# A two-layer graph network on one core: layer 2's partial sums kept in DRAM between the layers, in place of a second projection in layer 1

## The chip, the cores and the metric

The kernel runs on one core of one Trainium2 chip. The core has a matrix engine (TensorE; PE in the profile, with PEld for its weight loads), a vector engine (VectorE, DVE), a scalar engine (ScalarE, ACT), GpSimd (POOL), and SyncE (SP), which issues DMAs; 16 DMA engines move the data. Each engine works through its own instructions in program order and waits on semaphores. The metric is the time of one execution in microseconds (us), the median of several runs.

## The reference

There are N = 12500 nodes with 128 features and E = 200000 edges sorted by their target `dst`. Each edge has one of ten relations, the place of the largest of ten attributes. Both layers have the same form:

```python
def _rgcn_layer(x, src, dst, edge_type, w_rel, root, bias):
    N = x.shape[0]
    seg = dst * NUM_REL + edge_type
    xs = x[src]
    sums = jax.ops.segment_sum(xs, seg, num_segments=N * NUM_REL)
    cnt = jax.ops.segment_sum(jnp.ones(seg.shape, x.dtype), seg, num_segments=N * NUM_REL)
    mean = (sums / jnp.maximum(cnt, 1.0)[:, None]).reshape(N, NUM_REL, -1)
    return jnp.einsum('nrd,rdo->no', mean, w_rel) + x @ root + bias
...
h = jax.nn.relu(_rgcn_layer(x, src, dst, edge_type, w_rel1, root1, b1))
return _rgcn_layer(h, src, dst, edge_type, w_rel2, root2, b2)
...
x = _layernorm(x + _L0_gnn_ref(...), axis=-1)
```

So for each node and relation the rows of its neighbours are averaged, each average is multiplied by the relation's 128 x 128 matrix, and the ten results are added. Layer 2 does this with h, the rows that layer 1 gives. The sum over a node's edges may be split: the sums of two parts of the edges may be projected one by one, or added first and projected once.

## The kernel before, in words

**Tiles of edges.** The edges are cut into 1563 tiles of 128. For each tile GpSimd issues one indirect DMA (`gathered`, L751) that fetches the 128 source rows. VectorE builds one-hot columns for target and relation (`ones`, L765 for layer 1's edges, L768 for compacted ones), ScalarE weights them with 1 / count (`weighted`, L757), TensorE multiplies rows and one-hots into a PSUM bank `zp` (L978 in layer 1, L1480 in layer 2), and VectorE adds the bank into an accumulator `cc` (`sum_into`, L792) at a column that depends on the tile's first node.

**The accumulator.** `cc` is `[128, 2, 10, 1024 + 120]` floats: two rings, ten relations each, with one column for each of 1024 consecutive nodes (the columns after 1024 catch what runs over the end, and `folded` adds them to the beginning). As the nodes move on, a block of 256 nodes (128 or fewer near the end) that is complete is projected: `projected` multiplies the ten relations' columns by the ten weights (L739; one float product shows as two instructions) and adds one more product (L742). Then `cleared` (ScalarE, L722, two halves of five relations) writes zeros, and the same columns serve the nodes that lie 1024 further on.

**Layer 1 does part of layer 2.** From tile T0 = 166 on, the gather fetches from `XH`, a table that holds x and, for nodes whose h is ready, h next to it (zeros otherwise). So one gather of 1 KB rows feeds two products: x into ring 0 for layer 1, and h into ring 1 for layer 2. An edge whose source had its h in time is called seen. When a block k is complete, `finish` (L839) queues its steps at later positions of the tile loop, in units of four tiles: `rows_out` (bias, ReLU, transposition), `rows_kept` (h to `hD` and to `XH`), `second` (L876: projection of ring 1's sums over seen edges with layer 2's weights, and of h with its root matrix), `second_kept` (L879: bias by ScalarE, L883, and a store to `T2`, L884), the clears of both rings, and the next block's fetch.

**Layer 2** (`layer_2`, L1289) handles what is left: the first 166 tiles, and the unseen edges, which `brought_together` (L1058) sorts into 695 compacted tiles (using ring 0 as scratch, then zeroing it). These tiles form two walks, one from node 0 with ring 1, one from about node 6800 with ring 0, and a planner takes tiles from both in turn (`taken_in_turns`). Wide tiles are done in several passes over columns. `done_at` and `free_until` give the position at which a block is complete and at which its ring columns are needed again. `finish` (L1392) projects the block and adds the row of `T2` through a product with the identity (L742), `turn` transposes, `norm` adds x, normalises and stores `out`; two clears (8 and 12 units after the projection, a unit being 0.7 gathers for a block of 256 nodes) free the columns. `fetched` loads the block's rows of x and of `T2` on SyncE's queue. The block in which the walks meet (`partial`, `final`) goes through `T2` once more.

**Order.** The instructions are issued in the order written (a manual schedule). Waits follow from declared ranges: `offsets` (L773) reads a tile's column into a register and declares the range that it can have. A tile whose possible nodes lie on both sides of a multiple of 1024 is declared as the whole ring:

```python
lims = [limits(t0 + j) for j in range(n)]
lims = [(lo % RN, hi % RN) if lo // RN == hi // RN else (0, RN - 1) for lo, hi in lims]
```

A sum with a declared range waits for every earlier instruction or DMA that touches a column in it. There are 7 gather buffers of 8 rows each (a pair of x and h takes two), 6 for one-hots, and 3 (layer 2) or 5 (layer 1) PSUM banks for `zp`.

## Time and profile before

| | |
|---|---|
| median of 3 runs | 3114.19 us (3112.14 to 3119.51) |
| profiled execution, its own time | 3108.35 us |
| its span, first to last instruction | 3106.5 us |
| mean granted TensorE clock | 0.84 |
| layer 1's gathers | from the start to about 1958 us |
| layer 2's gathers | 1969.45 to about 3052 us |
| moved by DMA | 370.97 MB |

In the rows of groups, a name such as `zp<-oh,g` tells what is written from what; after `x` stands the number of instructions, then their busy time and the mean of one in ns, and behind the second bar the idle time of the engine just before them with what ended it ("issue": nothing that the profile shows). In the rows of windows each engine has its busy time and its number of instructions in brackets, in the order PE, PEld, DVE, ACT, POOL (a window of fewer engines or one line has those alone), then the granted clock, the DMA engines' busy share and GB/s. In a timeline the columns are start, duration, engine, line, operation, and in brackets the idle time before and what ended it. In the rows of waits stand the total, the number and the longest.

### The profile page before, as it was taken

What the parts mean: (1) busy time and instruction counts of PE and PEld (TensorE: products, weight loads), DVE (VectorE), ACT (ScalarE), POOL (GpSimd) and SP (SyncE); (2) the same over time, 40 slices, a digit from 0 to 9 for tenths busy, and PEclk for the clock granted to TensorE, in tenths of its full rate; (3) what the DMA queues carried; (4) which work ended last, traced back from release to release, by engine and by line L of the source; (5) the groups of instructions that cost most, each with busy time, mean ns of one, the idle gap of its engine ahead of it and who ended that gap; (6) DMA issues with size and microseconds to landing.
All of it is one profiled execution on the core that took longest, in us unless ns stands there. A gap on an engine that the chain in (4) does not pass through costs nothing.

```text
span 3106.5 us, 42362 instructions
## 1 busy us (share of the span) xinstructions
PE 2368.2 (76%) x11861; PEld 1949.5 (63%) x11861; DVE 2031.1 (65%) x5465; ACT 1301.6 (42%) x3177; POOL 2295.8 (74%) x2436
## 2 busy tenths in 40 slices
PE   2768787888787878787878788546467777777887
PEld 1556677777776767676767677545445555555665
DVE  6764657665656767655646464597776676777766
ACT  3533443433333434333433333332434455555643
POOL 7777777777777777777777777677777777777772
PEclk8768888888888889888888888767788888998988
DMA  6874444444545454545454444322222222222221
GB/s 191 270 216 143 141 145 141 140 146 122 161 122 162 124 157 129 159 122 160 125 158 127 128 121 118 95 59 62 64 67 68 72 73 74 72 73 73 79 73 43
DMA packets 265199, 370.97 MB, mean 119 GB/s; under 512 B 51232, under 2 KB 197189, under 8 KB 264958
## 3 DMA queue, kind: packets, MB, share of 16 engines
q0 software_dynamic: 99920, 250.57, 29.4%
q1 hardware_dynamic: 111347, 91.97, 9.4%
q10 hardware_dynamic: 53691, 25.62, 2.8%
q8 instruction: 102, 1.67, 0.2%
q14 instruction: 139, 1.14, 0.1%
HBM read 322.86 MB, written 57.89 MB: 123 GB/s over the span
## 4 chain that ended last, share of the span: by engine, by line
PE 30%; POOL 22%; issue 19%; DVE 14%; DMA 10%; ACT 2%; DVEq 1%; ACTq 0%; POOLq 0%; SPq 0%
POOL g L751 22%; PE pf L739 13%; DMA g<-XH,idxE 9%; PE zp L978 8%; PE zp L1480 6%; DVE cc L792 5%; DVE oh L768 2%; PE pf L742 1%; DVE cc L1158 1%; DVEq L777 1%; ACT cc L722 1%; ACT oh L757 1%; DVE oh L765 1%; DVE st L703 1%; DVE go L1146 1%
## 5 line engine op out<-in xcount | busy, mean ns | idle before, releaser
L751 POOL DMA_INDIRECT g<-XH,idxE x1397 | 1321.2, 946 | 425.6 <-issue 384.8
L792 DVE TENSOR_TENSOR cc<-cc,zp 128x240 f32 (+13 forms) x2500 | 959.8, 384 | 777.8 <-PE zp L978 388.2
L978 PE MATMUL zp<-oh,g 128*128 128x120 f32 x5920 | 983.2, 318 | 370.5 <-DMA g<-XH,idxE 206.8
L978 PEld LDWEIGHTS zp<-oh,g 128*128 128x128 f32 x5920 | 866.5, 222 | 487.2 <-issue 184.8
L751 POOL DMA_INDIRECT g<-hD,idxB x695 | 657.3, 946 | 215.9 <-issue 195.3
L739 PE MATMUL pf<-cc,w 128*128 128x256 f32 (+4 forms) x3000 | 732.1, 405 | 18.9 <-DVE cc L792 15.1
L1480 PE MATMUL zp<-oh,g 128*128 128x120 f32 (+23 forms) x1874 | 507.3, 415 | 284.4 <-DVE cc L792 156.4
L739 PEld LDWEIGHTS pf<-cc,w 128*128 128x128 f32 x3000 | 610.4, 215 | 121.1 <-DVE cc L792 22.5
L1480 PEld LDWEIGHTS zp<-oh,g 128*128 128x128 f32 x1874 | 338.9, 227 | 430.9 <-issue 271.0
L757 ACT ACTIVATE oh<-oh,wE 128x120 f32<-128x120 f32 x1729 | 530.9, 383 | 186.0 <-DVE oh L765 139.4
L757 ACT ACTIVATE oh<-oh,wB 128x150 f32<-128x150 f32 (+23 forms) x771 | 339.1, 482 | 296.5 <-DVE oh L768 269.4
L722 ACT ACTIVATE cc<-zero 128x1280 f32<-128x1280 f32 (+3 forms) x274 | 336.6, 1231 | 85.3 <-DVE cc L792 81.5
L768 DVE TENSOR_TENSOR oh<-go,keyB 128x480 f32<-128x480 f32 (+20 forms) x476 | 260.3, 547 | 115.1 <-PE zp L1480 113.6
L672 ACT ACTIVATE a<-pf,b 128x256 f32<-128x256 f32 (+1 forms) x50 | 23.3, 465 | 580.6 <-PE pf L742 578.9
L765 DVE TENSOR_TENSOR oh<-bank,keyE 128x480 f32<-128x480 f32 x391 | 253.0, 647 | 0.0
L751 POOL DMA_INDIRECT g<-hD,idxE x166 | 158.8, 957 | 61.7 <-issue 46.0
L751 POOL DMA_INDIRECT g<-in_x_dram,idxE x166 | 156.9, 945 | 52.2 <-issue 47.9
L883 ACT ACTIVATE v<-pf,b 128x256 f32<-128x256 f32 (+2 forms) x52 | 23.9, 459 | 361.4 <-PE pf L742 333.2
L548 DVE TENSOR_TENSOR eqb<-bank,kh 128x1344 bf16<-128x1344 f32 (+2 forms) x65 | 100.4, 1549 | 2.4 <-PE pf L559 2.0
L557 PE MATMUL pf<-eqb,identb 128*128 128x512 bf16 (+2 forms) x130 | 58.9, 453 | 12.4 <-DVE eqb L548 12.4
L559 PE MATMUL pf<-eqb,identb 128*128 128x512 bf16 (+2 forms) x130 | 58.5, 450 | 0.0
L706 ACT ACTIVATE rstd<-mv,eps 128x2 f32<-128x2 f32 (+5 forms) x54 | 15.9, 295 | 83.8 <-DVE mv L704 83.3
(235 smaller groups left out, 1097.8 us busy)
## 6 DMA issues: line engine op xcount, KB each, us to landing
m<-in_edge_attr_dram SPq DMA_DIRECT2D x48, 672.0 KB
g<-XH,idxE POOLq DMA_INDIRECT x1397
XH<-in_x_dram ACTq DMA_DIRECT2D x24, 512.0 KB
XH<-zero ACTq DMA_DIRECT2D x24, 512.0 KB
XH<-hb SPq DMA_DIRECT2D x87, 128.0 KB
g<-hD,idxB POOLq DMA_INDIRECT x695
xb<-in_x_dram SPq DMA_DIRECT2D x72, 128.0 KB
out_dram<-o SPq DMA_DIRECT2D x47, 128.0 KB
```

Of the source, the lines that this page charges most:

```text
L548: nc.vector.tensor_tensor(eq[:p], kpP[:p, None, :R].to_broadcast([p, DB, R]), fore, op=ALU.is_equal)
L557: nc.tensor.matmul(pc[:p], identb[:p, :p], eq[:p, k:k + 4, L:], start=(d + k == 1), stop=False)
L559: nc.tensor.matmul(pc[:p], identb[:p, :p], back, start=False, stop=(d + k + 3 == L))
L722: nc.scalar.activation(cc[:, l, h * H:(h + 1) * H, o:o + n], zero[:, None, :n].to_broadcast([P, H, n]), AF.Copy)
L739: nc.tensor.matmul(po[:, :n], wsb[l][:, r, :], cc[:, l if ring is None else ring, r, o:o + n], start=(r == 0), stop=False)
L751: nc.gpsimd.indirect_dma_start(out=g[:, j * C:(j + n) * C], out_offset=None, in_=table, in_offset=bass.IndirectOffsetOnAxis(ap=idx, axis=0))
L757: nc.scalar.activation(s, s, AF.Copy, scale=w)
L765: nc.vector.tensor_tensor(o.rearrange("p (t m) -> p t m", m=m), cols[:, None, :m].to_broadcast([P, n, m]), keys[:, :, None].to_broadcast([ ...
L768: nc.vector.tensor_tensor(o.rearrange("p (t r n) -> p t r n", r=NREL, n=w), cols[:, None, :, :w].to_broadcast([P, n, NREL, w]), keys[:, :, ...
L792: nc.vector.tensor_tensor(s, s, z, op=ALU.add)
L978: nc.tensor.matmul(zp[:, a + l * KW:a + (l + 1) * KW], g[:, (slot[j] + l) * C:(slot[j] + l + 1) * C], oh[:, j * KW:(j + 1) * KW], start=Tr ...
L1480: nc.tensor.matmul(zp[:, j * m:(j + 1) * m], gt[:, b * C:(b + 1) * C], oh[:, j * m:(j + 1) * m], start=True, stop=True)
```

## The change

In layer 1 `second` and `second_kept` are gone. In their place `sums_kept`, three parts (12 gathers) after the block's projection, stores h as columns in `hT` and, for blocks that can have seen edges, the block's columns of ring 1 in `S2`, `[128, 10, N]` in DRAM, both on SyncE's queue.

In layer 2 the clears are gone. `sums_back` loads the columns of `S2` for the nodes 1024 further on into the projected block's place, 2 units after the projection. Ring 0 gets its first 852 nodes from `S2` once the sorting has zeroed it. The projection then covers all edges at once: it adds root times h in place of identity times `T2`, `turn` adds the bias, and `final` adds the other walk's part by one more product with the identity. `T2` holds that one part alone. Tiles of the pool `fin` for up to four groups of 128 rows become tiles for three (left out of the diff, as are the lines around).

```diff
--- before.py
+++ after.py
@@ -208,7 +208,8 @@
     hD = dram.tile([N, C], F32, name="hD")
     hT = dram.tile([C, N], F32, name="hT")
     XH = [dram.tile([N, 2 * C], F32, name=f"XH{i}") for i in range(2)]
-    T2 = dram.tile([C, N], F32, name="T2")
+    S2 = dram.tile([C, NREL, N], F32, name="S2")
+    T2 = dram.tile([C, YB], F32, name="T2")
     KD = dram.tile([1, L + NT * P + L], F32, name="KD")
     CN = dram.tile([1, NT * P], F32, name="CN")
     counts = dram.tile([RS, NPAD], F32, name="counts")
...
@@ -729,17 +730,16 @@
         nc.vector.tensor_tensor(s, s, e, op=ALU.add)
         nc.vector.memset(e, 0.0)
 
-    def projected(k, l, last, po=None, more=True, ring=None):
+    def projected(k, l, ring, lasts):
 
         n0, n, _ = block(k)
         o = n0 % RN
-        if po is None:
-            po = ps_f.tile([P, YB], F32, name="pf")
-        for r in range(NREL if more else 0):
-            nc.tensor.matmul(po[:, :n], wsb[l][:, r, :], cc[:, l if ring is None else ring, r, o:o + n],
-                             start=(r == 0), stop=False)
-        w, f = last
-        nc.tensor.matmul(po[:, :n], w, f[:, :n], start=not more, stop=True)
+        po = ps_f.tile([P, YB], F32, name="pf")
+        for r in range(NREL):
+            nc.tensor.matmul(po[:, :n], wsb[l][:, r, :], cc[:, ring, r, o:o + n],
+                             start=(r == 0), stop=(r == NREL - 1 and not lasts))
+        for i, (w, f, a, b) in enumerate(lasts):
+            nc.tensor.matmul(po[:, a:b], w, f[:, :b - a], start=False, stop=(i == len(lasts) - 1))
         return po
 
     def stored(hb, b, k):
@@ -845,16 +845,16 @@
                 fTs[k] = features_in(k, 0, xbs[k])
             u = QB if t < NT else 0
             folded(ALL, k, WN)
-            po = [projected(k, 0, (rsb[0], fTs[k]))]
+            n0, n, subs = block(k)
+            po = [projected(k, 0, 0, [(rsb[0], fTs[k], 0, n)])]
             both = starts[k + 1] > bounds(T0)[0] if k + 1 < NBLK else True
             reused = starts[k] + RN < N
             assert not reused or t + 7 * u <= (starts[k] + RN - OFF - WN) // STEP
 
             def rows_out(_):
-                a = po.pop()
-                a = fin_a.setdefault(k, shifted(a, k, 0))
+                a = shifted(po.pop(), k, 0)
                 pr = ps_f.tile([P, 4, C], F32, name="pf")
-                n0, n, subs = block(k)
+                hs.append(a)
                 for i, h in subs:
                     nc.tensor.transpose(pr[:h, i, :], a[:, i * P:i * P + h], ident)
                 po.append(pr)
@@ -873,29 +873,23 @@
                         when = t + 8 * QB if k < K0 else first_seen[k] + 2 * QB
                         todo_late.append((when, lambda t: stored(hb, 1 - first, k)))
 
-            def second(_):
-                po.append(projected(k, 1, (rsb[1], fin_a.pop(k)), more=both))
-
-            def second_kept(_):
-                n0, n, _ = block(k)
-                p2 = po.pop()
-                t2 = fin.tile([P, YB], F32, name="v")
-                nc.scalar.activation(t2[:, :n], p2[:, :n], AF.Identity, bias=bsb[1])
-                nc.sync.dma_start(T2[:, n0:n0 + n], t2[:, :n])
+            hs = []
+
+            def sums_kept(_):
+                nc.sync.dma_start(hT[:, n0:n0 + n], hs.pop()[:, :n])
+                if both:
+                    o = n0 % RN
+                    nc.sync.dma_start(S2[:, :, n0:n0 + n], cc[:, 1, :, o:o + n])
 
             todo.at(t + u, rows_out)
             todo.at(t + (1 if k == NBLK - 2 else 2) * u, rows_kept)
             if reused:
                 todo.at(t + 2 * u, lambda t: cleared(0, k, 0))
                 todo.at(t + 3 * u, lambda t: cleared(0, k, 1))
-            if k < NBLK - 1:
-                todo.at(t + (9 if k >= NBLK - 3 else 3) * u, second)
-                todo.at(t + (9 if k >= NBLK - 3 else 4) * u, second_kept)
-            else:
+            if k == NBLK - 1:
                 todo.run(t)
                 todo.run(END)
-                todo.at(t, second)
-                todo.at(t, second_kept)
+            todo.at(t + 3 * u, sums_kept)
             if both:
                 w = 10 if k >= NBLK - 3 else 5
                 todo.at(t + w * u, lambda t: cleared(1, k, 0))
@@ -914,14 +908,13 @@
                 def turned_kept(t):
                     n0, n, subs = block(k + 1)
                     pt = po.pop()
-                    fTs[k + 1] = fin.tile([P, 4 * P], F32, name="fT")
+                    fTs[k + 1] = fin.tile([P, 3 * P], F32, name="fT")
                     nc.scalar.activation(fTs[k + 1][:, :n], pt[:, :n], AF.Copy)
                 todo.at(t + u, fetch)
                 w = 2 if k == NBLK - 3 else 4
                 todo.at(t + w * u, turn)
                 todo.at(t + (w + 1) * u, turned_kept)
 
-        fin_a = {}
         todo_late = []
         xbs[0] = rows_in(0)
         fTs[0] = features_in(0, 0, xbs[0])
@@ -1382,12 +1375,26 @@
                 return
             n0, n, subs = block(k)
             tail = "e" if walk_of[k] or k == final else ""
-            if k != partial:
-                assert k != final or partial in ended
-                xbs[k] = (comp if tail else fin).tile([P, 4, C], F32, name="xb" + tail)
+            if k == partial:
+                fTs[k] = None
+                return
+            if k == final:
+                assert partial in ended
+                fTs[NB2] = comp.tile([P, ranges[-1][partial][1]], F32, name="fP")
+                nc.sync.dma_start(fTs[NB2], T2[:, :ranges[-1][partial][1]])
+            if True:
+                xbs[k] = (comp if tail else fin).tile([P, 3, C], F32, name="xb" + tail)
                 rows_dma(xbs[k], x, k, False)
-            fTs[k] = (comp if tail else fin).tile([P, 4 * P], F32, name="fT" + tail)
-            nc.sync.dma_start(fTs[k][:, :n], T2[:, n0:n0 + n])
+            fTs[k] = (comp if tail else fin).tile([P, 3 * P], F32, name="fT" + tail)
+            nc.sync.dma_start(fTs[k][:, :n], hT[:, n0:n0 + n])
+
+        def sums_back(l, a, b):
+
+            ring = 1 - l
+            while a < min(b, (shared[1], N)[l]):
+                e = min(b, (shared[1], N)[l], a // RN * RN + RN)
+                nc.sync.dma_start(cc[:, ring, :, a % RN:a % RN + e - a], S2[:, :, a:e])
+                a = e
 
         def finish(k, i):
 
@@ -1398,7 +1405,10 @@
             u = (1 if n > YB * 5 // 8 else 0.7) if i < NG else 0
             folded(slice(ring, ring + 1), k, max([b[6] for b, (lo, hi) in zip(bunches, reaches)
                                                   if b[0] == walk_of[k] and lo < n0 < hi] + [WN]))
-            po = [projected(k, 1, (ident, fTs[k]), ring=ring)]
+            lasts = [] if k == partial else [(rsb[1], fTs[k], 0, n)]
+            if k == final:
+                lasts.insert(0, (ident, fTs[NB2], n - ranges[-1][partial][1], n))
+            po = [projected(k, 1, ring, lasts)]
             following = turn_of[walk_of[k]]
             if k == partial:
                 following = turn_of[1][1:2]
@@ -1410,12 +1420,13 @@
                 following = []
 
             def turn(_):
-                a = fin.tile([P, YB], F32, name="a")
-                nc.scalar.activation(a[:, :n], po.pop()[:, :n], AF.Copy)
+                a = fin.tile([P, 3 * P], F32, name="a")
                 if k == partial:
-                    nc.sync.dma_start(T2[:, n0:n0 + n], a[:, :n])
+                    nc.scalar.activation(a[:, :n], po.pop()[:, :n], AF.Copy)
+                    nc.sync.dma_start(T2[:, :n], a[:, :n])
                     fetched(following[0])
                     return
+                nc.scalar.activation(a[:, :n], po.pop()[:, :n], AF.Identity, bias=bsb[1])
                 pr = ps_f.tile([P, 4, C], F32, name="pf")
                 for b, h in subs:
                     nc.tensor.transpose(pr[:h, b, :], a[:, b * P:b * P + h], ident)
@@ -1430,8 +1441,7 @@
             assert i < by, (k, i, by)
             todo.at(min(i + 6 * u, by), turn)
             if clear[k]:
-                todo.at(min(i + 8 * u, by), lambda i: cleared(ring, k, 0))
-                todo.at(min(i + 12 * u, by), lambda i: cleared(ring, k, 1))
+                todo.at(min(i + 2 * u, by), lambda i: sums_back(1 - ring, n0 + RN, n0 + n + RN))
             if k != partial:
                 todo.at(i + 10 * u, norm)
 
@@ -1486,10 +1496,13 @@
                 flagged()
                 flag = 0
             jobs.run(i)
+            if "ring" in ready and "sums" not in ready:
+                ready.add("sums")
+                sums_back(1, shared[1], shared[0] + RN)
             q = p - BE
             if q >= 0:
                 l, second, t0, n, w, c, whole = bunches[q]
-                assert not l or "ring" in ready
+                assert not l or "sums" in ready
                 for j in range(n):
                     t = t0 + j
                     if (second, t) not in offs:
```

10 lines of the change are left out of this document (5 added, 5 removed).

## The prediction

> **What bounds the kernel now.** I read the page first (parts 1, 5 and 3), then windows by stage, then the waits of GpSimd and of VectorE, then two timelines.
>
> ```profile
> span 3106.5 us, 42362 instructions
> PE 2368.2 (76%) x11861; PEld 1949.5 (63%) x11861; DVE 2031.1 (65%) x5465; ACT 1301.6 (42%) x3177; POOL 2295.8 (74%) x2436
> L751 POOL DMA_INDIRECT g<-XH,idxE x1397 | 1321.2, 946 | 425.6 <-issue 384.8
> L739 PE MATMUL pf<-cc,w 128*128 128x256 f32 (+4 forms) x3000 | 732.1, 405 | 18.9 <-DVE cc L792 15.1
> ...
> L883 ACT ACTIVATE v<-pf,b 128x256 f32<-128x256 f32 (+2 forms) x52 | 23.9, 459 | 361.4 <-PE pf L742 333.2
> ```
>
> No engine is full by its share of busy time. The gather row says why that misleads: each gather is 946 ns of work and 0.30 us of "issue" (425.6 / 1397), and while it issues nothing else holds GpSimd back. The windows of all engines over layer 1 (250 to 1900) and the steady part of layer 2, and GpSimd's waits over the whole span, say it again:
>
> ```profile
> 250.00:1900.00 1650.00, 1356.55 (x7515) 1175.37 (x7513) 1019.37 (x2728) 641.70 (x1655) 1247.85 (x1321) 0.85 0.48 139
> 2200.00:3051.00 851.00, 643.40 (x2518) 465.65 (x2519) 604.71 (x1724) 432.42 (x901) 640.41 (x678) 0.88 0.28 72
> POOL g L751 <- issue: 674.0, 2212, 0.3
> POOL g L751 <- PE zp L978: 24.7, 81, 0.3
> POOL g L751 <- PE zp L1480: 16.0, 39, 2.3
> POOL g L751 <- PE pf L742: 14.4, 11, 11.4
> ```
>
> 1650 / 1321 is 1.249 us for one gather, which is 0.946 + 0.30: in layer 1 GpSimd never stops. Its longest wait there is 0.3 us. So **layer 1 lasts as long as its gathers**, whatever TensorE does beside them, as long as TensorE keeps up (1356.55 of 1650 busy).
>
> Layer 2 is different. The last gather and the product that uses it:
>
> ```profile
> 3050.91 0.94 POOL L751 DMA_INDIRECT g<-hD,idxB  x1 [0.30 <-issue]
> 3089.70 0.58 PE L1480 MATMUL zp<-oh,g 128*128 128x250 f32 x2
> 1969.45 0.94 POOL L751 DMA_INDIRECT g<-hD,idxE  x1 [11.38 <-PE pf L742]
> 1976.53 1.93 PE L1480 MATMUL zp<-oh,g 128*128 128x120 f32 x10 [2.49 <-ACT oh L757]
> ```
>
> The first layer 2 product runs 7.1 us behind its gather, the last one 38.8 us behind. TensorE and VectorE have fallen behind the gathers, and after 3051 they still work for 55 us. **The end of the kernel is set by the consumers of layer 2**, not by GpSimd: time added to their chain moves the end, and time taken out moves it by up to 38.8 - 7.1 = 31.7 us, when GpSimd becomes the bound.
>
> **Layer 1: what goes and what comes.** The second projection goes: it is 20 of the instructions of L739 for each of the 48 blocks from node 1024 on, 960 of 3000, or 732.1 x 960 / 3000 = 234 us of TensorE, with the 52 `second_kept` of L883 (23.9 us of ScalarE). All of it lies beside the gathers, at 1.249 us each: I cost the removal at **0**. If that cover were not there, the 234 us would be the gain; the 0.3 us waits exclude it.
>
> In its place SyncE stores 128 x 10 x 256 floats for each block (1.31 MB; 11476 nodes x 5120 bytes = 58.8 MB in all), and the same comes back in layer 2.
>
> ```profile
> q1 hardware_dynamic: 111347, 91.97, 9.4%
> 100.00:250.00 150.00, 112.18 (x547) 90.90 (x546) 92.83 (x242) 68.66 (x191) 113.42 (x121) 0.78 0.75 226
> 1500.00:1750.00 250.00, 210.18 (x1130) 180.66 (x1131) 135.75 (x307) 94.11 (x244) 189.07 (x201) 0.83 0.47 135
> ```
>
> SyncE's queue moved 91.97 MB in 9.4% of 3106.5 us, 0.315 MB in a us, so one store takes 1.31 / 0.315 = 4.2 us of all 16 DMA engines and all stores 187 us, a tenth of layer 1: the share goes from 0.47 to about 0.57. At 0.75 the gathers ran at 150 / 121 = 1.24 us, as at 0.47. Behind the store wait `cleared(1, k)` on ScalarE, due 2 parts (8 gathers, 10 us) later, and any sum whose declared range covers the block; both have 4 to 7 us to lose at most, and the gather buffers hold 28 pairs, 35 us. **0** again; if a stall outlasted the 35 us, GpSimd would show it.
>
> **The seam.** Today three stores of T2 wait for the last second projections, and the loads for sorting the unseen edges stand behind them in SyncE's queue:
>
> ```profile
> 1969.59 5.21 SPq L884 DMA_DIRECT2D T<-v  x3
> 1976.37 0.83 SPq L1077 DMA_DIRECT2D cc<-in_src_dram  x2
> 1983.91 1.68 DVE L1095 SCALAR_TENSOR_TENSOR cc<-cc,seen_below,go 127x1408 bf16<-127x1408 int32 x1 [13.43 <-DMA cc<-in_src_dram]
> ```
>
> The wait of 5.2 us goes; three stores of sums come ahead of the loads instead (128, 128 and 84 nodes, 1.74 MB, 5.5 us). Between -5.2 and +5.5 I take **0**.
>
> **Layer 2: clears become loads.** The projection keeps its 10 + 1 products (root times h for identity times T2; the block `final` gets one more, 0.6 us). What changes is how a projected block's place in the ring is made ready for the nodes 1024 further on: two clears on ScalarE, some 6 and 8 gathers after the projection (8 and 12 units of 0.7), become one 1.31 MB load from SyncE, issued within 2 gathers of it. 44 blocks do this.
>
> The waits of layer 2 from 2200 to the end, and one block (nodes 5632 to 5887) on its timeline, show what the clears cost and what a sum waits for:
>
> ```profile
> L722 ACT ACTIVATE cc<-zero 128x1280 f32<-128x1280 f32 (+2 forms) x80 | 99.6, 1245 | 24.5 <-DVE cc L792 22.4 <-DVE dn L1254 2.1
> DVE oh L768 <- PE zp L1480: 113.6, 46, 5.4
> DVE cc L792 <- PE pf L739: 35.6, 7, 6.6
> DVE cc L792 <- ACT cc L722: 12.0, 15, 1.2
> PEld zp L1480 <- ACT oh L757: 77.7, 100, 4.5
> ...
> 3008.28 4.48 PE L739 MATMUL pf<-cc,w 128*128 128x256 f32 x20
> 3020.42 6.27 PE L739 MATMUL pf<-cc,w 128*128 128x256 f32 x20 [2.65 <-DVE cc L792]
> 3026.73 0.82 DVE L792 TENSOR_TENSOR cc<-cc,zp 128x230 f32 x2 [5.80 <-PE pf L739]
> 3029.92 1.27 ACT L722 ACTIVATE cc<-zero 128x1280 f32<-128x1280 f32 x1 [0.72 <-DVE cc L792]
> 3031.22 0.82 DVE L792 TENSOR_TENSOR cc<-cc,zp 128x230 f32 x2 [0.79 <-ACT cc L722]
> ```
>
> Removed: 99.6 us of ScalarE, which waits for others and is no bound. On the chain lie VectorE's 12.0 us behind clears, and a part of the 77.7 us for which TensorE waits for weighted one-hots. Clears are 99.6 of ScalarE's 432.4 busy us in that window, 23%; 23% of 77.7 is 18 us. Bounds: 0 and 77.7. As TensorE is not the bound in all of these places, I take half, 9. Together **-21 us**.
>
> Added: the sum at 3026.73 waits 5.80 us until the projection has read its block, and the one at 3031.22 for the clear, though both add elsewhere in the ring. `offsets` declares the whole ring for a tile whose nodes may straddle a multiple of 1024, and a compacted tile reaches up to 560 nodes. Such a sum will now wait for the load to land. Working through the planner's formulas for this input (`bounds2`, `done_at`, the order of the bunches): of the 44 loads, 7 are followed by such a sum within 3 or 4 gathers of the projection (blocks 10, 18, 22, 27, 31, 35, 39), 4 more within 5 to 7 (6, 14, 30, 43), the rest after 10 or more, 12 us, by when the load is in. The 7 waits on L739 above are as many. (That two of the kinds agree in number is support, not proof.)
>
> How long is a load? At least its 4.2 us of transfer; at most 7.5 us, the 1976.37 to 1983.91 of the source load, which shared the queues with the two others of its size:
>
> ```profile
> cc<-in_src_dram SPq DMA_DIRECT2D x1, 616.0 KB
> cc<-CN SPq DMA_DIRECT2D x1, 616.0 KB
> cc<-KD SPq DMA_DIRECT2D x1, 616.0 KB
> ```
>
> SyncE's issue and the gathers' share (0.28) come on top of the 4.2, so I take 6.0. Of this TensorE uses about 1 us for products whose results the three banks of `zp` can hold, which VectorE then needn't wait for; the rest is lost, because VectorE stands in order: behind the waiting sum are the next one-hots and the next norm, behind those ScalarE's weighting, TensorE's products and the release of the gather buffers. So 7 x 5 + 4 x 2 (the later sums have 3 us of cover) = **+43 us**. Ends: 7 x 3.2 + 0 = 22 and 11 x 7.5 = 83.
>
> The first loads of ring 0 (852 nodes, 4.4 MB, 14 us by the same rate) follow the sorting and are wanted only 40 gathers of the other walk later (50 us): 0.
>
> **Sum.** 0 + 0 + 0 - 21 + 43 + 1 = **+23 us** on the profiled execution's 3108.35 us (span 3106.5 and 1.85 around it), 3131. That execution lies 5.84 us below the median of the runs, 3114.19, which I take as the base: **3137 us**.
>
> **Rivals.**
>
> *Faster: the loads are never waited for.* If sums and loads are kept apart by their true places (by the planner's own limit, `free_until`, the places in the rings do not collide for 17 or more gathers), or the 6 us lie under other idle time (113.6 us of one-hots waiting for TensorE), only the clears' gain stays: 3114 - 21 = 3093, down to 3082 at the 31.7 us at which GpSimd is the bound. For: VectorE is idle a quarter of layer 2. Against: the 35.6 and 12.0 us of waits of just this kind.
>
> *Nothing.* Gain and wait cancel: 3114. For: all the work of layer 1 is covered, and the layer 2 terms are of one size with opposite signs.
>
> *Much slower.* The loads take 7.5 us or more, block all 11 places and delay x, h and output rows on SyncE's queue, which is in order: 83 - 0 = +83, 3197. It decides from the point where the wait exceeds the 3 us of cover of the later four. Against: layer 2's DMA share is 0.28.
>
> *The stalls cool TensorE.* The projection after a wait of 2.65 us took 6.27 us, the one without 4.48: 1.8 us more. If each of the 11 load waits makes one more projection slow, +20 on the sum: 3157. [...]
>
> **Chances.** Forecast 0.47 (own range 3122 to 3152), cooled TensorE 0.13, much slower 0.08, faster 0.20, nothing 0.12. The range runs from 3094 to 3184: at the low end the clears' gain alone, at the high end load waits near their upper bound with half of the clears' gain. About 0.2% (6 us) is what a measurement of this kernel tells from no change: faster 0.20, same 0.12, slower 0.68, the latter from the first three cases.
>
> **What would show it.** Right: 1.249 us for a gather in layer 1 with TensorE busy less; in layer 2 a new wait of VectorE's sums on the load of `cc` from S2, about 11 times and 4 to 6 us each; no wait on clears after 2200; the lag of the last product growing beyond 38.8 us, or GpSimd waiting more often for L1480. Wrong: layer 1 shorter or longer by over 6 us, load waits at many more or at no places, or a lag that falls towards 7 us.

## The result, and the profile after

The changed kernel takes 3163.27 us (median of 5 runs, 3161.51 to 3167.81), the kernel before, beside it, 3113.22 us (3110.39 to 3119.51): a ratio of 1.0161, with an interval of 1.0146 to 1.0175. The change makes the kernel 50 us slower; 23 us were forecast.

The page of the changed kernel, its busy times and three groups:

```profile
span 3165.9 us, 40344 instructions
PE 2252.7 (71%) x10797; PEld 1842.3 (58%) x10797; DVE 2030.3 (64%) x5465; ACT 1195.1 (38%) x3037; POOL 2299.4 (73%) x2436
L751 POOL DMA_INDIRECT g<-XH,idxE x1397 | 1324.0, 948 | 427.4 <-issue 387.4
L739 PE MATMUL pf<-cc,w 128*128 128x256 f32 (+5 forms) x2040 | 512.9, 413 | 17.7 <-DVE cc L792 15.0
```

The work of 960 projection instructions is gone (3000 to 2040 on L739), and nobody profits: the end is 59 us later in the profiled execution (which took 3167.81 us, 4.5 above its median, where that of before lay 5.8 below). The windows of layer 1 and of layer 2's steady part:

```profile
250.00:1900.00 1650.00, 1230.04 (x6596) 1062.18 (x6595) 1016.68 (x2724) 626.15 (x1613) 1247.23 (x1317) 0.78 0.57 172
2200.00:3051.00 851.00, 620.59 (x2361) 448.72 (x2361) 571.81 (x1651) 335.34 (x782) 618.58 (x655) 0.84 0.45 129
```

Layer 1 gathers as it did: 1317 gathers in 1650 us, where there were 1321, with 127 us less of TensorE beside them. In the same 851 us of layer 2 GpSimd comes 23 gathers less far (655 for 678), TensorE 157 instructions less, VectorE 73. What they wait for, from 2200 us to the end (line, waited for, total, number, longest):

```profile
DVE oh L768 <- PE zp L1490: 119.0, 47, 6.1
DVE cc L792 <- DMA cc<-S: 53.8, 10, 7.3
DVE cc L792 <- PE pf L739: 35.8, 7, 6.9
...
PEld zp L1490 <- ACT oh L757: 72.3, 93, 4.5
...
POOL g L751 <- PE zp L1490: 42.9, 32, 10.0
```

One row is new: ten sums waited 53.8 us for a load from `S2`. The row of waits on clears is gone, the others shown are nearly as long as before. GpSimd, which waited 13.9 us for layer 2's products in this stretch, now waits 42.9: the gather buffers fill up behind the consumers. Such a wait on the timeline (a late one, the block at nodes 5632), with the last gather and the product that uses it:

```profile
3078.99 0.82 DVE L792 TENSOR_TENSOR cc<-cc,zp 128x230 f32 x2 [5.80 <-PE pf L739]
3079.88 0.52 SPq L1396 DMA_DIRECT2D cc<-S  x1
3087.64 0.83 DVE L792 TENSOR_TENSOR cc<-cc,zp 128x230 f32 x2 [7.25 <-DMA cc<-S]
3088.72 1.87 PE L1490 MATMUL zp<-oh,g 128*128 128x230 f32 x4 [7.46 <-DMA g<-hD,idxB]
...
3085.68 0.94 POOL L751 DMA_INDIRECT g<-hD,idxB  x1 [0.30 <-issue]
3148.45 0.58 PE L1490 MATMUL zp<-oh,g 128*128 128x250 f32 x2
```

The sum waits 5.80 us for the projection to read the block, as before. Then SyncE issues the load, and the next sum waits 7.25 us, until the load has landed, where the clear of before had cost the sum in this place 0.79 us. TensorE stands 7.46 us behind it. (The trace puts TensorE's wait down to a gather. But products run far behind their gathers here, and this one starts 0.25 us after VectorE's sum has ended, at 3087.64 + 0.83: by that, it waited for the PSUM bank.) At the end the last product runs 62.8 us behind its gather (38.8 before), and that gather itself is 34.8 us later: together the 58.8 us by which the last product moved.

### The profile page after: what moved, and what is told of

Its sections match the earlier page's. It is cut to its first block, busy times and chain, and to the rows that moved or that the text cites. A ratio compares the mean times of both kernels' runs of the same rounds, so it can differ in the third digit from the quotient of the medians.

```text
span 3165.9 us, 40344 instructions
## 1 busy us (share of the span) xinstructions
PE 2252.7 (71%) x10797; PEld 1842.3 (58%) x10797; DVE 2030.3 (64%) x5465; ACT 1195.1 (38%) x3037; POOL 2299.4 (73%) x2436
## 4 chain that ended last, share of the span: by engine, by line
PE 30%; DVE 17%; DMA 17%; POOL 16%; issue 16%; DVEq 2%; ACT 2%; SPq 0%; ACTq 0%; POOLq 0%
POOL g L751 16%; PE pf L739 11%; DMA g<-XH,idxE 11%; PE zp L971 10%; PE zp L1490 7%; DVE cc L792 6%; DVE oh L768 2%; DMA S<-cc 2%; DMA cc<-S 2%; DVEq L777 1%; DVE oh L765 1%; DVE cc L1151 1%; PE pf L742 1%; DVE st L704 1%; DVEq L792 1%
## 5 line engine op out<-in xcount | busy, mean ns | idle before, releaser
L971 PE MATMUL zp<-oh,g 128*128 128x120 f32 x5920 | 1068.8, 337 | 514.4 <-DMA g<-XH,idxE 353.9
L971 PEld LDWEIGHTS zp<-oh,g 128*128 128x128 f32 x5920 | 941.0, 239 | 642.2 <-issue 270.2
L1490 PE MATMUL zp<-oh,g 128*128 128x120 f32 (+23 forms) x1874 | 523.8, 426 | 323.5 <-DVE cc L792 187.4
L1490 PEld LDWEIGHTS zp<-oh,g 128*128 128x128 f32 x1874 | 351.8, 234 | 474.0 <-issue 321.6
L739 PE MATMUL pf<-cc,w 128*128 128x256 f32 (+5 forms) x2040 | 512.9, 413 | 17.7 <-DVE cc L792 15.0
L739 PEld LDWEIGHTS pf<-cc,w 128*128 128x128 f32 x2040 | 425.2, 218 | 94.9 <-DVE cc L792 21.9
L723 ACT ACTIVATE cc<-zero 128x1280 f32<-128x1280 f32 (+1 forms) x186 | 227.4, 1226 | 317.5 <-DVE cc L792 163.1
L768 DVE TENSOR_TENSOR oh<-go,keyB 128x480 f32<-128x480 f32 (+20 forms) x476 | 260.5, 547 | 120.7 <-PE zp L1490 119.0
L751 POOL DMA_INDIRECT g<-hD,idxE x166 | 158.7, 956 | 62.1 <-issue 46.3
L912 ACT ACTIVATE fT<-pf 128x256 f32<-128x256 f32 (+1 forms) x50 | 18.4, 369 | 149.8 <-PE pf L905 139.2
```

The lines of the kernel that those rows point to most:

```text
L723: nc.scalar.activation(cc[:, l, h * H:(h + 1) * H, o:o + n], zero[:, None, :n].to_broadcast([P, H, n]), AF.Copy)
L739: nc.tensor.matmul(po[:, :n], wsb[l][:, r, :], cc[:, ring, r, o:o + n], start=(r == 0), stop=(r == NREL - 1 and not lasts))
L751: nc.gpsimd.indirect_dma_start(out=g[:, j * C:(j + n) * C], out_offset=None, in_=table, in_offset=bass.IndirectOffsetOnAxis(ap=idx, axis=0))
L768: nc.vector.tensor_tensor(o.rearrange("p (t r n) -> p t r n", r=NREL, n=w), cols[:, None, :, :w].to_broadcast([P, n, NREL, w]), keys[:, :, ...
L971: nc.tensor.matmul(zp[:, a + l * KW:a + (l + 1) * KW], g[:, (slot[j] + l) * C:(slot[j] + l + 1) * C], oh[:, j * KW:(j + 1) * KW], start=Tr ...
L1490: nc.tensor.matmul(zp[:, j * m:(j + 1) * m], gt[:, b * C:(b + 1) * C], oh[:, j * m:(j + 1) * m], start=True, stop=True)
```

## The experiments

Theory A is the prediction's: loads +43 us, clears -21, the rest 0. Theory B: the sums' waits for the loads pass on to the end in full, and the clears were worth less. Theory C: the transfers themselves, or SyncE's queue, cost the time.

The runs whose kernel before takes 3111 to 3117 us, each against the kernel before beside it; the last column is the ratio's distance from 1, by 3113 us:

| label | kernel | us | ratio | interval | us against before |
|---|---|---|---|---|---|
| (after) | changed | 3163.27 | 1.0161 | 1.0146 to 1.0175 | +50 |
| t6_before_no_clears | before, no clears in layer 2 | 3099.22 | 0.9956 | 0.9942 to 0.9969 | -14 |
| e3_no_store | changed, no stores, loads, clears | 3101.72 | 0.9963 | 0.9949 to 0.9976 | -12 |
| s1_no_refill | changed, no loads, clears | 3106.76 | 0.9970 | 0.9958 to 0.9982 | -9 |
| t4_side_loads | changed, loads to another place | 3106.77 | 0.9982 | 0.9973 to 0.9991 | -6 |
| s5_placed_loads | changed, 11 loads moved | 3157.77 | 1.0132 | 1.0110 to 1.0155 | +41 |
| t8_before_placed_clears | before, clears moved | 3103.96 | 0.9974 | 0.9965 to 0.9983 | -8 |

**The clears by themselves.** In the kernel before:

```diff
-            if clear[k]:
-                todo.at(min(i + 8 * u, by), lambda i: cleared(ring, k, 0))
-                todo.at(min(i + 12 * u, by), lambda i: cleared(ring, k, 1))
```

> The kernel before without the 88 clears of layer 2 and with nothing in their place (so later nodes add to old sums). It sizes by itself the term that the prediction put at -21 us (12 us of VectorE's waits on clears and 9 of TensorE's waits for weighted one-hots). Theory A: 3093 us. Theory B, after the runs without loads and clears (3107 us with the stores, 3102 without, against 3114 to 3117 before): the waits on clears go and little else, 12 us less, 3101 to 3106 us, and TensorE's 77.7 us of waiting for weighted one-hots stay above 72.

It took 3099.22 us, 14 less than the kernel before (10 to 18 by the interval): 6 us above theory A's time and 2 below theory B's range. Its waits from 2200 us on:

```profile
DVE oh L768 <- PE zp L1477: 116.0, 50, 6.0
DVE cc L792 <- PE pf L739: 34.0, 7, 6.5
...
PEld zp L1477 <- ACT oh L757: 76.9, 98, 4.5
```

The 12.0 us of sums behind clears are gone. TensorE's waits for weighted one-hots stayed, 76.9 us for 77.7, as theory B had it, although ScalarE had 99.6 us less to do: of the prediction's two terms the first, 12, is there, the second, 9, is not.

**Layer 1 alone.** The changed kernel without loads and clears, and the same without the stores:

```diff
             if clear[k]:
-                todo.at(min(i + 2 * u, by), lambda i: sums_back(1 - ring, n0 + RN, n0 + n + RN))
...
-                sums_back(1, shared[1], shared[0] + RN)
```

```diff
                 if both:
-                    o = n0 % RN
-                    nc.sync.dma_start(S2[:, :, n0:n0 + n], cc[:, 1, :, o:o + n])
```

> The changed kernel without loads of S2 and without clears in layer 2 (the seen edges are left out and old sums stay in the ring). Against the kernel without stores (3102 us) it measures the stores, against the kernel with the clears back the clears, against the changed kernel the loads. Theory A (loads +43, clears -21): 3093 to 3098 us, 20 below the kernel with clears. Theory B (loads' waits in full, clears nothing): within 5 us of the kernel with clears, and 3102 + 5 = 3107 us if the stores cost layer 1 its 5 us.

> The changed kernel without loads of S2, without clears in layer 2 and without the stores of layer 1's sums to S2 (the seen edges are left out). Beside the same kernel with the stores it tells what layer 1's 5 us come from. If the stores' traffic slows the gathers or holds SyncE's queue: layer 1's last gather comes some 5 us sooner. If it is the lower TensorE clock (0.78 against 0.85 before): no difference, granted clock again near 0.78. The prediction's term for the stores was 0.

With the stores -9 us, without them -12; the intervals overlap, so no cost of the 58.8 MB of stores is shown (2 us, with some 6 to either side). The last gather of layer 1 starts at 1958.06 us without the stores; in the four kernels with them it starts between 1958.33 and 1961.98, so the 5 us for which that run was made are not settled. The waits in layer 1 behind the stores are there and hide: in the changed kernel ScalarE's clears of ring 1 wait 152.8 us for them, the sums 77.3 (over the whole span).

```profile
DVE cc L792 <- DMA S<-cc: 77.3, 10, 9.7
ACT cc L723 <- DMA S<-cc: 152.8, 36, 6.0
```

Against the kernel before without clears (-14), which is the same in layer 2, the kernel with the stores differs by 4 us: all that layer 1, the seam, and the new source of root times h add, within the intervals. And theory A's -20 between clears and no clears has no room: the kernel with neither loads nor clears is 9 us below before, not 21.

**The transfers without the waits.** Each load of a block goes to another tensor in DRAM, from the same place in SyncE's program and with the same bytes read:

```diff
+    S3 = dram.tile([C, NREL, N], F32, name="S3")
...
-                todo.at(min(i + 2 * u, by), lambda i: sums_back(1 - ring, n0 + RN, n0 + n + RN))
+                todo.at(min(i + 2 * u, by), lambda i: beside(1 - ring, n0 + RN, n0 + n + RN))
...
+                nc.sync.dma_start(S3[:, :, a:e], S2[:, :, a:e])
```

> The changed kernel with each of layer 2's 44 per-block loads sent to another place in DRAM and not into the ring (so layer 2 gets the seen edges of ring 0's first nodes only, and old sums stay): the same issue place on SyncE's queue, the same 1.31 MB read, written to DRAM; no sum waits for any of them. Beside a kernel before that takes 3114 us: theory B (the waits of sums behind a load cost the time) 3106 to 3114 us, as without loads (3107); theory C (the transfers slow the gathers, or the queue is held up) 3140 to 3165 us, though no sum waits for a load. In between, each has its share by the difference to 3107 and 3163.

3106.77 us. The window of layer 2 and the rows of waits (lines are one to eight further on in this kernel):

```profile
2200.00:3051.00 851.00, 643.02 (x2532) 466.82 (x2533) 609.08 (x1754) 357.10 (x835) 643.61 (x681) 0.88 0.50 135
...
DVE oh L769 <- PE zp L1498: 119.2, 52, 6.0
DVE cc L793 <- PE pf L740: 35.8, 7, 6.9
DVE cc L793 <- issue: 31.5, 31, 1.8
...
POOL g L752 <- PE zp L1498: 9.8, 32, 0.3
```

The DMA engines are busier than in the changed kernel (0.50 for 0.45), yet the window holds 681 gathers, as many as without any load (680), and no sum waits for a transfer. The changed kernel has ten waits, 53.8 us, that this one has not, and the ratios differ by 0.0179, 56 us (some 5 to either side). Two more things set the kernels apart. First, the copies don't wait for the projection to read its block, as the loads do (from 2200 us on SyncE's queue waits 158.7 us in 30 waits for the projections' last products, L742, before it issues them), so its queue should be held less; but from 2200 us on no other engine of the changed kernel waits for a transfer, the loads of `S2` and a few gathers (11.5 and 4.6 us) aside. Second, the copies aren't written into `cc`; but a sum takes 384 ns in the mean in both kernels, and a gather of a compacted tile 947 ns with the loads, 946 with the copies. With that, theory C falls.

**Moving the loads.** Nothing is left out here; 11 blocks' loads go to a place (in gathers) after which the next whole-ring sum should be 9 or more gathers off.

```diff
-                todo.at(min(i + 2 * u, by), lambda i: sums_back(1 - ring, n0 + RN, n0 + n + RN))
+                loads.at(min(i + late.get(k, 2 * u), by), lambda i: sums_back(1 - ring, n0 + RN, n0 + n + RN))
...
+            loads.run(i)
```

> The changed kernel, whole, with the loads of 11 of the 44 blocks (2, 6, 10, 14, 18, 22, 27, 31, 35, 39, 43) issued 14 to 56 gathers after the projection instead of 1.4, where no whole-ring sum follows for 9 or more gathers; the other 33 as they were. Theory B (what counts is a whole-ring sum right behind the load): the ten waits of 2 to 7 us (53.8 us) fall to one or two, and the time, from 3163 us, to 3106 to 3120 us. Theory C (the traffic, or SyncE's queue held up by 1.31 MB loads, costs the time): 3150 to 3165 us, as the transfers are all still there.

A miss: 3157.77 us, inside the range that theory C had there. But the waits did not go:

```profile
DVE cc L792 <- DMA cc<-S: 47.4, 7, 9.1
...
2306.07 13.26 SPq L1397 DMA_DIRECT2D cc<-S  x2
2311.64 0.44 DVE L792 TENSOR_TENSOR cc<-cc,zp 128x270 f32 x1 [4.85 <-DMA cc<-S]
```

The passes over a wide tile share one gather number, so a load placed by gathers can still land ahead of the passes it was to follow, as at 2306. By the planner's formulas seven of the 11 moved loads (blocks 6, 10, 14, 27, 31, 35, 39) are still issued right ahead of a sum whose declared range covers them, and the seven waits stand at sums of just these widths. Seven waits of 47.4 us, 6.4 less than the changed kernel, and the time is 5.5 us less (9 by the ratios). That agrees with theory B; the run doesn't separate it from C, the one before does.

**The version that beats both.** The kernel before, its clears placed by the number of the bunch, away from whole-ring sums:

```diff
-                todo.at(min(i + 8 * u, by), lambda i: cleared(ring, k, 0))
-                todo.at(min(i + 12 * u, by), lambda i: cleared(ring, k, 1))
+                for h in range(2):
+                    clears.at(places[k][h], lambda p, h=h: cleared(ring, k, h))
...
+            clears.run(p)
```

(`places` holds two bunch numbers for each block.)

> The kernel before, whole, with layer 2's clears issued by the number of the bunch in the program, at places that no whole-ring sum of the same ring stands close before or behind, beside a kernel before that takes 3114 us. The kernel before without any clears takes 14 us less; its trace shows the 12.0 us of sums waiting for clears gone and the waits for weighted one-hots as they were. If the waits are the whole of the clears' price: 3099 to 3106 us, with under 4 us of sums waiting for clears. If the price is ScalarE's 99.6 us of work and not the waits: 3110 to 3115 us though the waits fall.

3103.96 us, 8 us (5 to 11) below the kernel before. In its waits no row of sums behind clears is left, and the waits for weighted one-hots are as they were. In their place TensorE's weight loads wait 7.3 us for clears (0.5 before). ScalarE still does all 274 clears:

```profile
DVE cc L792 <- PE pf L739: 35.6, 7, 7.0
DVE cc L792 <- issue: 32.4, 31, 1.9
...
PEld zp L1481 <- ACT oh L757: 78.1, 104, 4.4
...
PEld zp L1481 <- ACT cc L722: 7.3, 6, 2.3
...
L722 ACT ACTIVATE cc<-zero 128x1280 f32<-128x1280 f32 (+3 forms) x274 | 336.1, 1230 | 64.9 <-DVE cc L792 63.1 <-issue 1.0 <-PE pf L739 0.7
```

So most of the clears' 14 us was their place. Whether the other 6 us are ScalarE's work, as the new row suggests, or spread between runs isn't settled: the intervals of the two kernels touch.

**Runs beside a kernel before that takes 4001 to 4044 us.** In these the kernel before itself takes that long, and not some 3114 us. One of them, `e6_before_no_clears`, in its window of layer 1 and in TensorE's waits over the whole span:

```profile
250.00:1900.00 1650.00, 1057.63 (x5694) 931.32 (x5692) 812.39 (x2269) 496.66 (x1281) 952.09 (x1005) 0.76 0.38 112
...
PE zp L978 <- issue: 675.6, 496, 23.2
```

There are 1005 gathers in place of some 1320, each of them as long as ever (952.09 / 1005 = 947 ns), and TensorE's products wait 675.6 us for nothing that the profile shows (73.0 in the kernel before at 3114 us). So layer 1 isn't bound by its gathers there; what else holds it stays open. Therefore these ratios answer another question and aren't mixed with those above:

| kernel | labels and ratios |
|---|---|
| before, no clears | e6_before_no_clears 1.0019, r6_before_no_clears 1.0024 |
| before, clears moved | s8_before_placed_clears 1.0014 |
| changed, clears in place of loads | e2_clears_back 1.0063, r2_clears_back 1.0075, s2_clears_back 1.0065 |
| changed, loads to another place | s4_side_loads 1.0093 |
| changed, no loads, no clears | e1_no_refill 1.0102, r1_no_refill 1.0107 |
| changed, 11 loads moved | e5_placed_loads 1.0133, r5_placed_loads 1.0153 |
| changed, 15 loads moved, by bunch | s7_placed_by_bunch 1.0139 |

The intervals are some 0.002 to either side. None of the times forecast for these runs, all made for a kernel before of some 3114 us, could be tried there. For the kernel before without clears and with moved clears:

> The kernel before, without the 88 clears of layer 2 and with nothing in their place (so the later nodes add to old sums; ScalarE does 99.6 us less there). It measures by itself the term that the prediction put at -21 us. Theory A (the prediction's term is right): 3113 - 21 = 3092 us, with the last product less than 38.8 us behind its gather. Theory B (the clears lie beside idle time; the 12 us of waits on them turn into waits for the next thing): 3108 to 3115 us, and the 77.7 us that TensorE waits for weighted one-hots hardly fall.

> The kernel before without the 88 clears of layer 2, once more, where the kernel before takes 3114 us. Theory A (the prediction's -21 is right): 3092 us, the last product less than 38.8 us behind its gather. Theory B (the clears lie beside idle time): 3108 to 3115 us, and the 77.7 us that TensorE waits for weighted one-hots hardly fall.

> The kernel before, whole, with layer 2's clears issued by the number of the bunch in the program, at places that no whole-ring sum of the same ring stands close before or behind (2.5 us or more where there is such a place). The kernel before without any clears takes 14 us less than before; its trace shows the 12.0 us of sums waiting for clears gone and the waits for weighted one-hots as they were. If the waits are the whole of the clears' price: 3099 to 3106 us, with under 4 us of sums waiting for clears. If the price is ScalarE's 99.6 us of work and not the waits: 3110 to 3115 us though the waits fall.

For the changed kernel without loads and clears, and with its loads sent elsewhere or moved:

> The changed kernel without loads of S2 and without clears in layer 2 (the seen edges are left out and old sums stay in the ring). Against the kernel with the clears back it measures the clears once more, against the changed kernel the loads. Theory A: loads +43, clears -21, so 3093 to 3098 us, 20 below the kernel with clears. Theory B: the same as the kernel with clears within 5 us, 3110 to 3120 us; no wait of VectorE's sums on any transfer into cc, and the last product some 40 us behind its gather. Theory C: above 3140 us.

> The changed kernel without loads of S2 and without clears in layer 2 (the seen edges are left out), once more where the kernel before takes 3114 us. Against the kernel without stores (3102 us) it measures the stores, against the kernel with the clears back the clears, against the changed kernel the loads. Theory A: 3093 to 3098 us, 20 below the kernel with clears. Theory B: within 5 us of the kernel with clears, and 3102 + 5 = 3107 us if the stores cost layer 1 its 5 us.

> The changed kernel with each of layer 2's 44 per-block loads sent to another place in DRAM and not into the ring (so layer 2 gets the seen edges of ring 0's first nodes only, and old sums stay): the same issue place on SyncE's queue, the same 1.31 MB read by the same packets, written to DRAM; no sum waits for any of them. Theory B (the waits of sums behind a load cost the time): 3106 to 3114 us, as without loads (3107). Theory C (the transfers slow the gathers, or the queue is held up): 3140 to 3165 us, though no sum waits for a load. In between, each has its share by the difference to 3107 and 3163.

> The changed kernel, whole, with the loads of 11 of the 44 blocks (2, 6, 10, 14, 18, 22, 27, 31, 35, 39, 43) issued 14 to 56 gathers after the projection instead of 1.4, at a place that is followed by no whole-ring sum for 9 or more gathers; the other 33 as they were. Theory B (what counts is a whole-ring sum right behind the load): the ten waits of 2 to 7 us (53.8 us) fall to one or two, and the time to 3108 to 3122 us. Theory A: the same waits go, so 3163 - 50 = 3113 us or, if the clears' gain is then felt, down to 3095 us. Theory C (the traffic, or SyncE's queue held up by 1.31 MB loads, costs the time): 3150 to 3165 us, as the transfers are all still there.

> The changed kernel, whole, with the loads of 11 of the 44 blocks (2, 6, 10, 14, 18, 22, 27, 31, 35, 39, 43) issued 14 to 56 gathers after the projection instead of 1.4, where no whole-ring sum follows for 9 or more gathers, once more where the kernel before takes 3114 us. Theory B (what counts is a whole-ring sum right behind the load): the ten waits of 2 to 7 us (53.8 us) fall to one or two, and the time to 3106 to 3120 us. Theory C (the traffic, or SyncE's queue held up by 1.31 MB loads, costs the time): 3150 to 3165 us, as the transfers are all still there.

Two kernels have no other run. The first is the changed kernel with the two clears of before in place of each load:

> The changed kernel with the two clears of before (8 and 12 units after the projection) in place of each load, and no load of S2 at all (so layer 2 leaves the seen edges out). Layer 1 and everything else is as changed. The prediction's terms: 0 for layer 1 and the seam, clears as before, no loads: 3113 to 3115 us. Theory B, in which the loads' waits pass on in full and layer 1 is some 5 us longer: 3163 - 54 + 5 - 0, that is 3113 to 3120 us. Theory C (the loss lies elsewhere: the h columns fetched, the bias in turn, the longer layer 1): above 3140 us.

> The changed kernel with the two clears of before in place of each load, and no load of S2 at all (layer 2 leaves the seen edges out), once more where the kernel before takes 3114 us. The prediction's terms (0 in layer 1, 0 at the seam, clears as before): 3113 to 3115 us. Theory B (layer 1 some 5 us longer, the loads' waits pass on in full): 3113 to 3120 us. Theory C (the loss lies elsewhere than in the loads): above 3140 us. The kernel without stores, loads and clears took 3102 us: if the stores cost layer 1 its 5 us and the clears some 10, this one comes to 3117 us.

> The changed kernel with the two clears of before (8 and 12 units after the projection) in place of each load, and no load of S2 at all (layer 2 leaves the seen edges out). The prediction's terms (0 in layer 1, 0 at the seam, clears as before): 3113 to 3115 us, 20 above the kernel with neither. Theory B (layer 1 some 5 us longer, clears worth nothing): within 5 us of the kernel with neither. Theory C (the loss lies elsewhere than in the loads): above 3140 us.

The second places the loads by the bunch, `loads.at(lands[k], ...)` and `loads.run(p)`:

> The changed kernel, whole, with the loads placed by the number of the bunch of tiles in the program, not by the number of gathers: in the first placed kernel several passes over a wide tile share one gather number, so seven loads still stood right ahead of a whole-ring sum, and those seven waits cost 47.4 us, as much as the ten of the changed kernel. Here the loads of 15 blocks are moved so that the next whole-ring sum follows 8 us or more after the place in the program is reached (5.7 to 7 us for blocks 30 and 34). Theory B (a sum that must wait for the load is what costs the time): at most three waits on the load, together under 8 us, and 3106 to 3118 us in place of 3158. Theory C (the transfers or SyncE's queue cost it): 3145 to 3165 us though the waits go.

A miss: its waits on loads were 30.9 us in 7, where at most three under 8 us were expected, and it stands where the first placed kernel does. How far moved loads can bring the changed kernel down stays open. In one point the order agrees with the above: the loads to another place cost no more than no loads at all. In another it doesn't: with clears the changed kernel is faster here than without (1.0063 to 1.0075 for 1.0102 and 1.0107), which nothing above explains.

## Why the prediction was wrong, point by point

**Layer 1 at 0: held.** The gathers ran at 1650 / 1317 = 1.253 us (1.249 forecast as the sign of it), TensorE had 127 us less to do in the window, and GpSimd's longest wait for products of layer 1 stayed at 0.3 us. Without loads and clears the change is worth -9 us where the clears alone are worth -14, so layer 1, stores and seam together cost some 4 us, which lies within the intervals. The single profile shows the last layer 1 gather 4.9 us later (1961.98 for 1957.12), and the kernel with moved loads, the same in layer 1, only 1.2 us (1958.33): the difference of 3.7 us lies between executions.

```profile
1961.98 0.94 POOL L751 DMA_INDIRECT g<-XH,idxE  x1 [0.30 <-issue]
...
1957.12 0.95 POOL L751 DMA_INDIRECT g<-XH,idxE  x1 [0.30 <-issue]
```

(The first row is the changed kernel's, the second that of before.)

**The clears at -21: too much.** Measured by itself -14. The 12 us of VectorE's waits behind clears did go, and account for most of it. The 9 us for half of ScalarE's share of the one-hot waits did not: those waits stayed (77.7 to 76.9) when the clears went. Reading ScalarE's share of busy time into a wait was the mistake; the row names ScalarE as releaser, but ScalarE itself waits for VectorE's one-hots there, 269.4 us in layer 2 before, 311.1 without the clears: part of its freed time turned into longer waits for its input.

```profile
ACT oh L757 <- DVE oh L768: 269.4, 269, 8.7
...
ACT oh L757 <- DVE oh L768: 311.1, 345, 8.7
```

**The load waits at +43: the place was right, the size too small.** Whole-ring sums right behind a load were named as the mechanism, at 11 blocks; ten waits appeared. The largest part of the miss is this term: 53.8 us of waits, and 56 us (0.0179 of 3113) between the kernel that has them and the one that has the same transfers without them. The step that failed is the price of one wait, the "7 x 5 + 4 x 2", in three places.

- The load itself: 6.0 us were taken for it. From its issue to the start of the sum that waited for it 6.9 us passed in the mean (5.4 to 7.9).
- The "3 us of cover" of the later four: the widths of the waiting sums tell the blocks apart. By them the sums behind the seven near places waited 41.4 us in all (35 forecast), and those behind three of the later four, blocks 6, 43 and 14 below, 12.4 us (8 forecast). Behind block 30 no sum waited.
- The sentence "Of this TensorE uses about 1 us for products whose results the three banks of `zp` can hold": nothing of the kind came off, as 53.8 us of waits cost 56 us (with 1 us off each of the ten it would have been 44).

```profile
2483.98 0.31 DVE L792 TENSOR_TENSOR cc<-cc,zp 128x150 f32 x1 [4.07 <-DMA cc<-S]
2780.44 0.53 DVE L792 TENSOR_TENSOR cc<-cc,zp 128x360 f32 x1 [6.08 <-DMA cc<-S]
2860.89 0.34 DVE L792 TENSOR_TENSOR cc<-cc,zp 128x180 f32 x1 [2.23 <-DMA cc<-S]
```

So a wait of VectorE's counted in full, 5.4 us in the mean (53.8 / 10). That fits with VectorE as the engine that is late in layer 2: its other waits didn't shrink in exchange (119.0 us for 113.6 on `zp`, 35.8 for 35.6 on the projection).

**The extra transfers at 0: held**, some 4 us (-9 without, -6 with them), within the intervals.

So, by the runs: -14 (clears) + 4 (layer 1, stores and seam) + 4 (transfers) + 56 (waits) = +50; the forecast was -21 + 0 + 0 + 43 + 1 = +23. (The four are differences along one chain of runs, so that they add up to 50 is no test of them.) The two parts that were off, 7 and 13, have one sign, and the two fours, neither beyond its intervals, make up the rest.

**The rivals.** *Faster* needed loads that nobody waits for: that kernel exists, it is the one with the loads to another place, and it is faster by 6 us, not 21. *Much slower* had the right form (waits in full, near 83 us) and too many places. *The stalls cool TensorE* came nearest in time (3157), and TensorE did slow down by what it priced, though not where it was priced. From 2200 us on the same 2681 instructions kept TensorE busy for 702.60 us in place of 682.71, 19.9 us more where 20 were priced. Of these 3.7 lie in the projections (224.59 for 220.86), 15.1 in the products (461.69 for 446.60). All engines, the projections and the products (of each pair before first, then changed; the rows of one line have TensorE and its weight loads alone):

```profile
2200.00:3166.00 966.00, 682.71 (x2681) 497.16 (x2681) 638.80 (x1833) 450.86 (x944) 641.27 (x678) 0.88 0.25 65
...
2200.00:3166.00 966.00, 702.60 (x2681) 512.75 (x2681) 642.44 (x1852) 371.75 (x869) 645.66 (x683) 0.84 0.42 122
...
2200.00:3166.00 966.00, 220.86 (x920) 182.51 (x920) 0.88 0.25 65
...
2200.00:3166.00 966.00, 224.59 (x920) 185.18 (x920) 0.84 0.42 122
...
2200.00:3166.00 966.00, 446.60 (x1562) 285.00 (x1562) 0.88 0.25 65
...
2200.00:3166.00 966.00, 461.69 (x1562) 297.05 (x1562) 0.84 0.42 122
```

The end doesn't show these 20 us on top of the waits: the waits on loads are 53.8 of the 56 us, and VectorE waits for products no longer than in the kernel whose loads go elsewhere (119.0 us for 119.2). So the slower TensorE lies for the most part beside VectorE's work. The granted clock did fall, from 0.88 to 0.84, as this rival has it. From 2200 to 3051 us it is 0.84 in the changed kernel and in the one with 11 loads moved, whose sums wait for loads, and 0.87 to 0.89 in the kernel before and the five others of the first table. The prediction's two projections differ in the same way: over their own time in the kernel before the clock was 1.00 in the faster one (4.48 us from 3008.28) and 0.73 in the one behind the wait of 2.65 us (6.27 us from 3020.42). So a lower clock goes with the waits here; what links the two, no run shows.

## What to carry to other kernels

When a short operation on a shared buffer becomes a DMA, ask which later instruction of an in-order engine has a declared range that covers it: the true places didn't help here, and each such instruction paid what was left of the transfer, 2.2 to 7.3 us, at a DMA share of 0.45. A wait of the engine that is late is best counted in full (here 53.8 us of them cost 56), and an engine's freed time at nothing until its own waits have been read (ScalarE's 99.6 us left the one-hot waits at 76.9 us for 77.7). To find out whether a transfer or a wait costs the time, send the same transfer somewhere nobody looks.

## What was not expected of the hardware

In layer 1 less work made the rest slower. With the second projection gone, the granted clock fell from 0.85 to 0.78, and the 5920 products of the other kind went from 318 ns to 337; without the stores too they take 346 at 0.76:

```profile
L978 PE MATMUL zp<-oh,g 128*128 128x120 f32 x5920 | 983.2, 318 | 370.5 <-DMA g<-XH,idxE 206.8
...
L971 PE MATMUL zp<-oh,g 128*128 128x120 f32 x5920 | 1068.8, 337 | 514.4 <-DMA g<-XH,idxE 353.9
...
250.00:1900.00 1650.00, 1320.36 (x6597) 1110.07 (x6597) 1021.93 (x2724) 622.41 (x1607) 1248.19 (x1319) 0.76 0.48 139
L968 PE MATMUL zp<-oh,g 128*128 128x120 f32 x5920 | 1138.9, 346 | 417.0 <-DMA g<-XH,idxE 304.1 <-issue 34.1 <-DVE cc L792 26.7
```

(The kernel before first, then the changed kernel, then the one without stores, loads and clears.) All five kernels without the second projection that ran beside a kernel before of some 3114 us show it, with 0.76 to 0.78 and 336 to 346 ns; the three that keep it (the kernel before, without clears, and with moved clears) have 0.85 and 318 or 319 ns. So a part of the work taken from a TensorE that isn't the bound came back as a lower clock: 919 instructions went from the window, 224 us at the 244 ns that one took before (732.1 / 3000), and TensorE is 127 us less busy there. Here it hides beside the gathers; what it would do to a kernel near TensorE's limit, no run shows.
